# Layer 2's g product of a fused four-layer network: 128-column stationary tiles against pairs of 64-column tiles

## The chip, the cores and the metric

The kernel runs on one core of a Trainium2 chip. The metric is the device time of one execution in microseconds; the time before is the median of three runs. The engines are called PE (matrix products, with PEld for its weight loads), ACT, DVE, POOL and SP (whose queue issues most DMAs). A matrix product has a stationary operand (the "weight", loaded by LDWEIGHTS) and a moving operand that streams through the array; a shape such as 128\*64 after an instruction's name gives rows and columns of the part of the array that it uses, and 128x64 after that the moving operand. Each product of fp32 operands appears in the trace as two records (two passes), each with a weight load of its own.

## The reference

The input x is 4 samples of 256 channels of 48 x 48 pixels (N = 2304 pixels), fp32. Four layers follow one another, each adding its result for the group-normalised x to x: an attention with 8 heads of 64 (layer 0), a gate from max pooling and strip convolutions (layer 1), a non-local block (layer 2), and a channel gate with a 3 x 3 depthwise convolution (layer 3). The change lies in layer 2:

```python
xt = x.reshape(b, c, h * w)
theta_x = jnp.einsum('oc,bcn->bno', theta_w, xt) + theta_b
phi_x = jnp.einsum('oc,bcn->bon', phi_w, xt) + phi_b[:, None]
g_x = jnp.einsum('oc,bcn->bno', g_w, xt) + g_b
f = jnp.einsum('bnc,bcm->bnm', theta_x, phi_x) * c1 ** (-0.5)
attn = jax.nn.softmax(f, axis=-1)
y = jnp.einsum('bnm,bmc->bnc', attn, g_x)
```

theta, phi and g have 64 output channels each. g_x has the pixels in its rows, so its product takes the pixels of x as the stationary operand (transposed) and the weight g_w, 256 x 64, as the moving one.

## The kernel before, in words

Channels lie in 128 partitions and NK = 2 halves. Pixels are worked on in slices of SL = 384 (NSL = 6 to a sample). The order of the instructions on every engine is written out by hand: `attend` walks over groups of an attention unit (9 groups of two 128-pixel tiles each), and in each group records, in this order, the score products of the group (`scores`, L324, evicted by ACT with an exponential at L330 into `pt`), the jobs that fall due in it (`due`, `fills`, with ranks that order them), the "other" lanes of work (layer 1, norms), and the value products of the group before (`weigh`, L344). DVE and POOL add up the `pt` tiles (L370, L364; L355 on POOL). Layer 0 runs 16 phases of 6 units, layer 2 then 4 phases of 3 units.

`project2(b, norm, s2)` makes layer 2's operands of sample b. Per slice s it has two jobs:

- `both(s)`: theta and phi in one product of 128 output columns (L1199, two channel halves accumulated in one `pj` tile of PSUM), evicted by ACT in two halves (L1205, L1209), with a DMA copy of phi (L1213).
- `g(s)`: three tiles of 128 pixels, each the sum over two channel halves, into one `pj` tile (L1220); ACT copies the 128 x 192 result to `s2["v"]` (L1225). For sample 0 the next slice of x is fetched by a DMA afterwards (L1193).

`pj` tiles have two buffers, shared with every other small product: the output projection of layer 0 (`out_proj`, L723, two parts, read by DVE at L739), the sums of the softmax (`total`, L383, copied by ACT at L388; `total_here`, L429 in the last sample), the group means (L233, L247), and the per-channel statistics (L1255, read by DVE at L1263). A third tile of products can thus be begun only when the first has been read.

The jobs of the six slices are placed as follows. Sample 0: in the last phase of layer 0, one slice in each unit, in the order `both`, first part of the output projection, `g`, second part, `total`. Samples 1 and 2: in the layer-2 phase before, two slices at a time, in the order `both`, `both`, `g`, `g`. Sample 3: drained in one go at the end of sample 2's phase, slice by slice (`follow`), near 3190 to 3208 us in the trace. The start of `project2` computes biases, with two products into halves of the partitions (L1169, weights of 128 x 64, one moving column). Beside the layer-2 phases of samples 0 to 2, layer 1 of the last sample runs, on DVE (maxima, L890 to L922), PE (L1061), POOL and SP.

Of the kernel before, what the change touches and what calls it, by code (L numbers as in the profile page):

```python
# [14 lines left out]
P = 128  # L15
HW = 48
N = HW * HW
NK = 2
HEADS = 8
D = 64  # L20
# [58 lines left out]
def usual_path(  # L79
    tc, x, wqkv, wout, vecs, dww, thphi_w, thphi_b, g_w, g_b, W_w, attn_w1, attn_w2, refine_w, out  # L80
):
    nc = tc.nc
# [13 lines left out]
    def pj_tile():  # L96
        return ps_pj.tile([P, 512], F32, tag="pj", name="pj")
# [217 lines left out]
    HALVES = (slice(0, D), slice(D, P))  # L315
# [835 lines left out]
    def project2(b, norm, s2):  # L1151

        at = {}

        def start():
            kd = big.tile([P, N], F32, tag="k", name="kd")
            qv = big.tile([P, N], F32, tag="q", name="qv")
            s2["k"], s2["q"] = kd, qv[:, 0:HALF]
            s2["v"] = qv[:, HALF:N].rearrange("p (j d) -> p j d", d=D)
            ps = pj_tile()  # L1160

            for k in range(NK):
                nc.tensor.matmul(
                    ps[:, 0:1], lhsT=w2c[:, k, 0:2, :].rearrange("p t d -> p (t d)"),
                    rhs=norm["nb"][:, k : k + 1], start=k == 0, stop=k == NK - 1,
                )
            for c in HALVES:
                for k in range(NK):
                    nc.tensor.matmul(  # L1169
                        ps[c, 1:2], lhsT=w2c[:, k, 2, :],  # L1170
                        rhs=norm["nb"][:, k : k + 1], start=k == 0, stop=k == NK - 1,
                    )
            bias = small.tile([P, 2], F32, tag="bias2", name="bias2", bufs=3)
            nc.vector.tensor_add(bias, ps[:, 0:2], b2c)
            s2["shift"] = bias[:, 1:2]
            w = wqp.tile([P, NK, 3, P], F32, tag="w", name="w2")
            w = w.rearrange("p k t o -> p k (t o)")[:, :, : 3 * D]
            w = w.rearrange("p k (t d) -> p k t d", d=D)
            for k in range(NK):
                nc.scalar.activation(  # L1180
                    w[:, k], w2c[:, k], AF.Identity, scale=norm["rs"][:, k : k + 1]
                )
            if b:
                at["x"] = lambda s, k: X[b][:, k, s * SL : (s + 1) * SL]
            else:
                at["x"] = lambda s, k: at[s][:, k, :SL]
                fetch(0)
                fetch(1)
            at["w"], at["bias"] = w, bias

        def fetch(s):
            at[s] = xsp.tile([P, NK, SL + 1], F32, tag="xs", name="xs2")
            nc.sync.dma_start(at[s][:, :, :SL], x_out[:, :, s * SL : (s + 1) * SL])  # L1193

        def both(s):

            ps = pj_tile()[:, :SL]
            for k in range(NK):
                nc.tensor.matmul(  # L1199
                    ps, lhsT=at["w"][:, k, 0:2, :].rearrange("p t d -> p (t d)"),  # L1200
                    rhs=at["x"](s, k), start=k == 0, stop=k == NK - 1,
                )
            phi, theta = HALVES
            cols = slice(s * SL, (s + 1) * SL)
            nc.scalar.activation(  # L1205
                s2["k"][phi, cols], ps[phi], AF.Identity, bias=at["bias"][phi, 0:1]
            )
            c = s % L2C
            nc.scalar.activation(  # L1209
                s2["q"][HALVES[s // L2C], c * SL : (c + 1) * SL], ps[theta], AF.Identity,  # L1210
                bias=at["bias"][theta, 0:1],
            )
            nc.sync.dma_start(s2["k"][theta, cols], s2["k"][phi, cols])  # L1213

        def g(s):
            ps = pj_tile()
            nj = SL // P
            for i in range(nj):
                for k in range(NK):
                    nc.tensor.matmul(  # L1220
                        ps[:, i * D : (i + 1) * D],
                        lhsT=at["x"](s, k)[:, i * P : (i + 1) * P],
                        rhs=at["w"][:, k, 2, :], start=k == 0, stop=k == NK - 1,
                    )
            nc.scalar.copy(  # L1225
                s2["v"][:, s * nj : (s + 1) * nj, :].rearrange("p j d -> p (j d)"),
                ps[:, : nj * D],
            )
            if b == 0 and s + 2 < NSL:
                fetch(s + 2)  # L1230

        return start, [
            [(1, lambda s=s: both(s)), (2 if b else 2.7, lambda s=s: g(s))] for s in range(NSL)
        ]

# [225 lines left out]
    for i, (b, p) in enumerate(order):  # L1461
# [13 lines left out]
        else:  # L1475
            start, slices = project2(0, norms2[0], twos[0])
# [28 lines left out]
    for b in range(B):  # L1505
# [12 lines left out]
        if b + 1 < B:  # L1518
            spread(work, stats(b, 0), [22, 23])
            start, slices = project2(b + 1, norms2[b + 1], twos[b + 1])  # L1520
# [6 lines left out]
            at = [s for s in range(n) if s in work or s % NG == AT_TOTAL]  # L1527
# [147 lines left out]
    for k in range(NK):  # L1675
# [7 lines left out]
        of_groups, lhsT=gmat, rhs=means.rearrange("p b k -> p (b k)"), start=True, stop=True  # L1683
# [1350 lines left out]
```

## Time and profile before

| what | value |
|---|---|
| median of 3 runs | 3460.08 us (3459.35 to 3461.13) |
| profiled execution, own time | 3461.47 us |
| its span, first to last instruction | 3459.7 us |
| mean granted TensorE clock | 0.996 |
| PE busy | 3397.6 us (98%) |
| ACT, DVE, POOL busy | 66%, 73%, 24% |
| L1199 (`both`), PE busy | 35.7 us, 96 records |
| L1220 (`g`), PE busy | 35.3 us, 288 records |
| where L1220 runs | 2707 to 3208 us |

In the lines of the groups, the columns are the source line, the engine, the operation, the tiles written and read, the shape, the count, then busy time in us and the mean of one instruction in ns, then the idle time of the engine before them and what ended it. In the lines of a timeline, the first number is the start in us from the start of the span and the second the time that the merged instructions cover; the bracket gives idle time before and the releaser. A matrix product's recorded duration holds its latency, so the pace of a stream is read from the starts and not from the durations.

### The profile page before, as it was taken

Reading aid. Unit: us, or ns where it says so; the run is one execution under the profiler, and the core shown is the slowest. Engines: PE = TensorE matmul, PEld = TensorE weight load, DVE = VectorE, ACT = ScalarE, POOL = GpSimd, SP = SyncE. Lnnn points to the kernel's source line nnn. Section 1 sums busy time; section 2 is a strip of 40 time slices with the busy share of each in tenths; the row PEclk is TensorE's granted clock in tenths of the full one; section 3 lists DMA queues with packets and bytes.
Section 4 is the critical chain, followed back from the end, with each engine's and each line's share of the span. In section 5 each row is a group of like instructions: output and inputs, shape, how many; then the busy total and the mean of one; then the engine's idle time right before and its main releaser. Section 6 shows DMA issues by size and latency. Waiting matters only on the chain. (4 is left out here: it accounts for less than half of the span.)

```text
span 3459.7 us, 88715 instructions
## 1 busy us (share of the span) xinstructions
PE 3397.6 (98%) x37678; PEld 1711.7 (49%) x37678; DVE 2540.6 (73%) x3298; ACT 2297.1 (66%) x3690; POOL 824.9 (24%) x734
## 2 busy tenths in 40 slices
PE   8999999999999999999999999999999999899988
PEld 5555545555545444545454445554544444445533
DVE  3455545568788788687888787878887878857777
ACT  5565556565886687557866875568758855444577
POOL 2433333320011011101110010111011105776434
PEclk9999999999999999999999999999999999999999
DMA  2211111111111111121111110111111110221067
GB/s 91 49 23 27 22 27 22 27 22 27 21 32 22 27 22 27 27 72 22 27 22 27 15 31 15 31 18 31 18 28 17 30 21 9 59 62 11 8 152 230
DMA packets 111590, 127.20 MB, mean 37 GB/s; under 512 B 42912, under 2 KB 101648, under 8 KB 110416
## 3 DMA queue, kind: packets, MB, share of 16 engines
q1 hardware_dynamic: 109936, 119.53, 17.1%
q8 instruction: 297, 4.87, 0.6%
q10 hardware_dynamic: 1248, 1.91, 0.2%
q14 instruction: 109, 0.89, 0.1%
HBM read 56.99 MB, written 11.80 MB: 20 GB/s over the span
## 5 line engine op out<-in xcount | busy, mean ns | idle before, releaser
L330 ACT ACTIVATE pt<-sc 128x768 f32<-128x768 f32 x1944 | 1473.4, 810 | 759.8 <-PE sc L324 753.3
L370 DVE TENSOR_TENSOR acc<-acc,pt 128x768 f32<-128x768 f32 x1368 | 1367.1, 999 | 145.5 <-ACT pt L330 51.8
L344 PE MATMUL av<-pt,v 64*64 64x384 f32 x13824 | 1274.9, 484 | 0.0
L324 PE MATMUL sc<-q,k 64*64 64x384 f32 x13824 | 1270.1, 482 | 0.5 <-ACT pt L330 0.5
L324 PEld LDWEIGHTS sc<-q,k 64*64 64x64 f32 x13824 | 525.4, 133 | 589.6 <-issue 556.5
L344 PEld LDWEIGHTS av<-pt,v 64*64 64x64 f32 x13824 | 518.2, 133 | 568.4 <-issue 521.5
L421 POOL TENSOR_TENSOR o<-o,rinv 128x384 f32<-128x384 f32 x95 | 120.3, 1267 | 1712.4 <-DMA rinv<-rinv 1702.4
L355 POOL TENSOR_TENSOR half<-pt 128x768 f32<-128x768 f32 x189 | 369.0, 1957 | 495.2 <-ACT pt L330 417.0
L739 DVE SCALAR_TENSOR_TENSOR x<-pj,bo,x 128x384 f32<-128x384 f32 x192 | 118.5, 617 | 346.3 <-ACT row L388 188.0
L951 ACT ACTIVATE prod<-pd,wt 128x256 f32<-128x256 f32 x486 | 340.7, 761 | 0.2
L370 DVE TENSOR_TENSOR acc<-acc,half 128x768 f32<-128x768 f32 x171 | 187.6, 1097 | 169.4 <-POOL half L355 168.2
L625 PE MATMUL pj<-xs,w 128*128 128x384 f32 (+1 forms) x720 | 275.4, 505 | 0.0
L625 PEld LDWEIGHTS pj<-xs,w 128*128 128x128 f32 x720 | 124.1, 189 | 127.9 <-ACT v L664 34.3
L974 DVE TENSOR_REDUCE prod<-prod 128x256 f32<-128x1280 f32 x114 | 168.7, 1480 | 0.9 <-ACT prod L951 0.9
L344 PE MATMUL av<-pt,qv 64*64 64x384 f32 x1728 | 169.0, 495 | 0.0
L324 PE MATMUL sc<-qv,kd 64*64 64x384 f32 x1728 | 165.3, 487 | 2.3 <-ACT pt L330 2.2
L723 PE MATMUL pj<-o,wo 128*128 128x384 f32 (+1 forms) x384 | 161.3, 502 | 1.1 <-DVE x L739 0.8
L364 DVE TENSOR_TENSOR acc<-pt 128x768 f32<-128x768 f32 x99 | 119.7, 1209 | 39.3 <-ACT pt L330 39.1
L659 PEld LDWEIGHTS pj<-w,xs 128*128 128x128 f32 x1080 | 134.4, 191 | 24.2 <-issue 1.2
L659 PE MATMUL pj<-w,xs 128*128 128x128 f32 x1080 | 134.9, 275 | 0.0
L417 POOL TENSOR_TENSOR o<-raw 128x384 f32<-128x384 f32 x95 | 120.8, 1271 | 45.9 <-ACT raw L413 44.7
L413 ACT COPY raw<-av 128x768 f32<-128x768 f32 x108 | 86.4, 800 | 48.3 <-PE av L344 47.8
(304 smaller groups left out, 2256.4 us busy)
## 6 DMA issues: line engine op xcount, KB each, us to landing
xs<-in_x_dram SPq DMA_DIRECT2D x90, 384.0 KB
sh<-pad SPq DMA_DIRECT2D x126, 162.2 KB
rinv<-rinv SPq DMA_DIRECT2D x208, 94.5 KB
out_dram<-x SPq DMA_DIRECT2D x23, 384.0 KB
w<-in_wqkv_dram SPq DMA_DIRECT2D x32, 192.0 KB
x<-in_x_dram SPq DMA_DIRECT2D x4, 1152.0 KB
x<-in_x_dram SPq DMA_DIRECT2D x9, 384.0 KB
rinv<-ls SPq DMA_DIRECT2D x208, 1.5 KB
```

The lines of the kernel that those rows point to most:

```text
L324: nc.tensor.matmul(ps[c * D : (c + 1) * D, h, :SL], lhsT=u["of"]["k"][r, j0 : j0 + D], rhs=u["of"]["q"][r, u["qc"]], start=True, stop=True,)
L330: nc.scalar.activation(pt, ps[:, :, :SL], AF.Exp, scale=u["scale"])
L344: nc.tensor.matmul(u["av"][h * D : (h + 1) * D, half, :SL], lhsT=value(u, j, h)[r], rhs=pt[r, h, :], start=j == 0, stop=j == JB - 1,)
L355: nc.gpsimd.tensor_add(half, pts[0], pts[1])
L370: nc.vector.tensor_add(u["acc"], u["acc"], term)
L417: eng.tensor_add(u["sum"], u["raw"][:, 0, :], u["raw"][:, 1, :])
L421: eng.tensor_mul(o, o, u["rinv"])
L625: nc.tensor.matmul(ps[:, :n], lhsT=at["w"][:, k, t, :], rhs=xs[s][:, k, :n], start=k == 0, stop=k == NK - 1,)
L659: nc.tensor.matmul(ps[:, i * P : (i + 1) * P], lhsT=xs[s][:, k, i * P : (i + 1) * P], rhs=at["w"][:, k, 2, :], start=k == 0, stop=k == NK - 1,
L723: nc.tensor.matmul(ps[:, :n], lhsT=wo[:, p, k * P : (k + 1) * P], rhs=o["o"][:, :n], start=True, stop=True,)
L951: nc.scalar.activation(bufs[n % 3][:, :, min(n, 1) + i].rearrange("p (r c) -> p r c", c=AS), pd[:, PAD + dr : PAD + dr + AS, PAD + dc : PA ...
L974: nc.vector.tensor_reduce(to, bufs[n % 3][:, :, : min(n, 1) + len(taps)], AX.X, ALU.add)
```

## The change

In `g`, each stationary operand of 128 pixels is given as two stationary operands of 64 pixels, one after the other, with the same moving operand; the second writes PSUM partitions 64 to 127. `HALVES` is `(slice(0, 64), slice(64, 128))`. The sums, the `pj` tile and the copy that follows are as they were.

```diff
             for i in range(nj):
                 for k in range(NK):
-                    nc.tensor.matmul(
-                        ps[:, i * D : (i + 1) * D],
-                        lhsT=at["x"](s, k)[:, i * P : (i + 1) * P],
-                        rhs=at["w"][:, k, 2, :], start=k == 0, stop=k == NK - 1,
-                    )
+                    for c in HALVES:
+                        nc.tensor.matmul(
+                            ps[c, i * D : (i + 1) * D],
+                            lhsT=at["x"](s, k)[:, i * P + c.start : i * P + c.stop],
+                            rhs=at["w"][:, k, 2, :], start=k == 0, stop=k == NK - 1,
+                        )
```

## The prediction

> **What bounds the kernel now.** I read the page's engine table first, then the groups by shape for the edited line, then the timeline at each place where that line runs, and the waits of PE between those places.
>
> ```profile
> PE 3397.6 (98%) x37678; PEld 1711.7 (49%) x37678; DVE 2540.6 (73%) x3298; ACT 2297.1 (66%) x3690; POOL 824.9 (24%) x734
> L1220 PE MATMUL pj<-w,x 128*128 128x64 f32 x216 | 26.0, 275 | 0.0
> L1220 PE MATMUL pj<-w,xs 128*128 128x64 f32 x72 | 9.3, 279 | 3.7 <-ACT qv L1209 3.7
> ```
>
> PE sets the time. The edited line has 288 records: 24 calls of g with 12 each (three 128-pixel tiles, two channel halves, and two passes per fp32 product). They hold 35.3 us, so no more can be at stake. The trace starts one of them every 112 ns: in the next timeline 12 weight loads fill 1.42 us, and (1420 - 192) / 11 = 112. The moving part is only 64 columns, and 112 ns is also the pace of L659, which moves 128. So the load of a 128-column weight sets this pace. The 24 calls stand in three surroundings. The first, six times in the last phase of layer 0:
>
> ```profile
> 2707.03 0.58 ACT L1209 ACTIVATE qv<-pj,bias 64x384 f32<-64x384 f32 x1
> ...
> 2707.65 1.42 PEld L1220 LDWEIGHTS pj<-w,xs 128*128 128x128 f32 x12 [1.24 <-ACT qv L1209]
> 2707.66 1.55 PE L1220 MATMUL pj<-w,xs 128*128 128x64 f32 x12 [0.62 <-ACT qv L1209]
> 2708.99 0.30 PEld L723 LDWEIGHTS pj<-o,wo 128*128 128x128 f32 x2
> ```
>
> PE stands 0.62 us until ACT has evicted `both`, does g, and goes straight on to L723. The second, six pairs of calls in layer 2 (the first of two timeline fences), and the third, six calls drained one after another near 3200 us (the second):
>
> ```profile
> 2903.74 2.89 PE L1220 MATMUL pj<-w,x 128*128 128x64 f32 x24
> ...
> 2904.40 0.58 ACT L1209 ACTIVATE qv<-pj,bias 64x384 f32<-64x384 f32 x1
> ...
> 2906.56 0.21 PEld L344 LDWEIGHTS av<-pt,qv 64*64 64x64 f32 x8
> ```
>
> ```profile
> 3192.34 1.45 PE L1220 MATMUL pj<-w,x 128*128 128x64 f32 x12
> ...
> 3193.14 0.58 ACT L1209 ACTIVATE qv<-pj,bias 64x384 f32<-64x384 f32 x1
> ...
> 3193.77 1.56 PE L1199 MATMUL pj<-x,w 128*128 128x384 f32 x4
> ```
>
> In the pair, the second call may start when the second eviction ends, 2904.40 + 0.58 + 0.05 = 5.03 (counting from 2900); before, PE arrived at 5.13. In the third surrounding the next `both` starts 50 ns after ACT's L1209 ends: PE already waits for ACT there, whatever g takes.
>
> **What the Trainium skill says.** "TensorE: Matmul & The Clock Gate", section "LDWEIGHTS (loading the stationary operand)", prices a load by its columns over 1.2 GHz: 107 ns for 128 and 53 for 64. The trace's 112 agrees for 128, with some 5 ns of handover. "TensorEngine Tiling (Array Packing)", section "Key Properties", says that tiles load and multiply independently, and that a change of tiling drains the engine. Both show in the trace:
>
> ```profile
> 2701.75 0.32 PEld L1169 LDWEIGHTS pj<-gn_nb,w2c 128*64 128x64 f32 x8
> 2701.75 0.41 PE L1169 MATMUL pj<-gn_nb,w2c 128*64 128x1 f32 x8
> ...
> 3238.30 0.20 PEld L429 LDWEIGHTS pj<-acc,ones 128*64 128x64 f32 x4 [0.60 <-issue]
> 3238.31 0.87 PE L429 MATMUL pj<-acc,ones 128*64 128x384 f32 x4
> ```
>
> L1169 loads 128x64 weights into two column tiles: 8 loads of 138 ns in 0.32 us, in pairs 13 ns apart, one pair each (320 - 138 - 13) / 3 = 56 ns (58 between its products). In L429 the two halves stream 384 columns together (starts 7 ns apart, then 373 ns on). The drain: L383 of 128x32 tiles starts its last product at 2710.130, streams 96 columns for 80 ns, and the 64x64 tiles of L344 start loading at 2710.304, 94 ns later; L429 gives 94 as well. "TensorE: Matmul & The Clock Gate", section "The mechanism" under Part 3, says that a load overlaps running products only for another row group; L1169 and L659 (load and product of 107 ns each at a pace of 112) use the same rows and do overlap, so the measurement decides for me.
>
> **The change part by part.** Each call's 12 loads and products of 128*128 become 24 of 128*64, two column tiles side by side. PSUM contents, the copy L1225, ACT, DVE, POOL and the DMAs keep their number and order; only lines of PE grow (288 loads and 288 products more).
> - Inside a call, before: from first to last product 1277 ns (160 for the first, exposed load, then 10 x 111.7). After: 109 ns for the first interval (53 of exposed load and 56 of products), then 10 x 58, and 7 for the second half: 696. Saved: 581 ns. A 64-column pace between 56 (products) and 62 (some handover more) moves this by -20 to +40 ns.
> - Change of tiling on the way in: the drain of 94 ns ends before the eviction that g waits for (0.62 us of idle; in the pairs the load starts 465 ns after L1199's last product, the drain would allow it at 320 + 94 = 414). Cost nothing while that wait is there. Only the third surrounding has no such wait: 94 + 53 of exposed load.
> - On the way out: to L723 the next load may start 53 + 94 = 147 ns after the last product instead of 56: 91 lost, or 87 with rounding of the starts. To L344 (64x64) the drain is paid already: nothing.
>
> First surrounding: 581 - 87 = 494 ns a call. The fourth call is followed by L723 waiting for DVE's L739 until 2796.02, 0.24 us of idle, so its gain is lost: 5 x 0.494 = 2.47 us. PE's own later waits here (DVE L443 near 2882) hang on PE's L429 and move along.
>
> Pairs: before, from the first product to the last 1277 + 111 + 1229 = 2617 ns. After, the first call ends early but the second waits for the eviction, 5.03 - 3.74 = 1.29 us, and then takes 0.70: 1.99. Gain 0.63 us a pair, half of what the pair saves on PE. The pairs at 2903 and 2935 lie in a stretch where DVE has no gap from 2890.6 to 2984, but for some 0.1 us thrice, and PE waits for it after each:
>
> ```profile
> 2919.89 1.73 DVE L243 TENSOR_TENSOR gn_sq<-gn_sq,gn_mv 128x2 f32<-128x2 f32 x1
> ...
> 2921.68 0.38 PE L247 MATMUL pj<-gn_sq,gmat 128*128 128x2 f32 x2 [1.05 <-DVE gn_sq L243]
> ```
>
> ```profile
> 2952.16 1.25 PE L324 MATMUL sc<-qv,kd 64*64 64x384 f32 x12 [2.20 <-ACT pt L330]
> ```
>
> I take both gains as lost to these waits, which grow by 0.63 us. From 2984 on DVE itself waits for POOL's L355, which waits for ACT and so for PE, 15 times at L370 alone up to 3192: there a gain stays. Four pairs: 2.50 us.
>
> Third surrounding: five calls gain nothing (ACT's two evictions, 0.58 each, set the cycle of 2.83 us). The last is followed by L344: before, its last product starts 322 + 1173 = 1495 ns after L1199's last; after, 414 + 2 + 696 = 1112. Gain 0.38 us.
>
> Sum: 2.47 + 2.50 + 0.38 = 5.35 us. The profiled execution took 3461.47 us (span 3459.7, 1.8 around it), 1.4 above the median 3460.08 of the runs. It should become 3456.1; taken from the median, 3454.7. What the sum leaves out is the granted clock: after 2880 us the trace has six stretches at half clock (the shortest 3.41 us, the window that "TensorE: Matmul & The Clock Gate" gives in "What's actually happening"), a window each worth up to 1.7 us of PE, and a shift of PE can move one in or out. So 1.7 either way.
>
> **The rivals.**
> A, more arrives. DVE's L243 took 1.73 us for 128x2 while POOL ran L355 beside it (other DVE lines of that shape take 0.16). If such stretches end with POOL, whose start follows PE, the waits at 2921 and 2952 move along, and the two lost pairs come back; the fourth call of the first surrounding does too if DVE reaches L739 sooner: 5.35 + 1.25 + 0.49 = 7.1 us, 3453.0. For it: the length of L243. Against: DVE's row has no gap, so its backlog stays.
>
> B, less arrives. DVE's stretches beside POOL fall otherwise in the later pairs too and eat their 2.50: 2.85 us, 3457.2. Against it: 4 to 7 us gaps in DVE's row after 2984.
>
> C, slower. The halves don't overlap, since nothing in this trace alternates 64-column loads with products as short as 64 columns in column tiles. With load and product of both halves in a row, a pair costs 4 x 53 + 10 = 222 ns: a call takes 2.44 us. First surrounding 5 x 1.25 + 0.8; pairs 4 x 2.6, and 2.0 for the two whose waits take the rest; third 5 x 1.3 + 1.4: 27 us, 3487. It decides from about 108 ns a pair, where nothing is gained, and passes 0.2% at about 137. Loads alone in a row (117) would give about no change. Against it: L1169 and L429.
>
> **How the numbers follow.** 0.2% of the time, 6.9 us, is about what a measurement of this kernel can tell from no change. Forecast 0.46, A 0.33, B 0.13, C 0.08. With 1.7 us of clock either way, A passes 6.9 us in somewhat over half of its cases and the forecast in some 0.17 of its own: 0.22 + 0.08 = 0.30 faster. C gives slower nearly always, 0.08; the rest, 0.62, is within 0.2%. The range runs from A with the clock's gain and a little more of the saved 581 ns (9 us, 3451.0) to B with the clock's loss (3459.0); C and some ends of A lie outside.
>
> **What would show it.** L1220 as 128*64, 576 records, 24 of them in about 0.97 us with the last one's tail, pairs 58 ns apart; L723 loading 147 ns after the last product; PE waiting about 0.5 us for L1209 between the two calls of a pair; a cycle of 2.83 us unchanged near 3200; and waits at 2921 and 2952 longer by 0.6 (shorter ones speak for A). A pair interval over 100 ns makes the forecast wrong, and so does a wait of PE for DVE after 2984 that grows by a call's gain.

## The result, and the profile after

The changed kernel takes 3453.76 us in the median, the kernel before 3461.89 in the same comparison; the medians lie 8.1 us apart. The ratio, for which an interval is given, is 0.9979 (95%: 0.9973 to 0.9984), so 7.3 us faster (5.5 to 9.3). The forecast was 5.35. The profiled execution took 3453.34 us with a span of 3451.5, 8.2 shorter than the profiled span before.

From the page's engine table and the groups by shape (samples 1 to 3 of the edited line, now L1221):

```profile
PE 3384.6 (98%) x37966; PEld 1698.6 (49%) x37966; DVE 2539.3 (74%) x3298; ACT 2297.4 (67%) x3690; POOL 828.0 (24%) x734
L1221 PE MATMUL pj<-w,x 128*64 128x64 f32 x432 | 16.5, 226 | 2.2 <-ACT qv L1209 2.2
```

PE has 288 products more and is busy for 13.0 us less. Before, half as many records of these samples filled 26.0 us. The last entry is new: PE now waits for ACT's L1209 inside the pairs. The timelines of the three surroundings, first the first call in layer 0's last phase:

```profile
2708.17 0.78 PEld L1221 LDWEIGHTS pj<-w,xs 128*64 128x64 f32 x24 [1.24 <-ACT qv L1209]
2708.18 0.92 PE L1221 MATMUL pj<-w,xs 128*64 128x64 f32 x24 [0.62 <-ACT qv L1209]
2709.02 0.30 PEld L723 LDWEIGHTS pj<-o,wo 128*128 128x128 f32 x2
```

24 loads in 0.78 us where 12 took 1.42; the idle of 0.62 ahead is as before, and L723 loads 0.85 us after the first load, not 1.34. Then a pair in layer 2, and the drained calls:

```profile
2900.83 0.58 ACT L1209 ACTIVATE qv<-pj,bias 64x384 f32<-64x384 f32 x1
...
2901.46 0.92 PE L1221 MATMUL pj<-w,x 128*64 128x64 f32 x24 [0.37 <-ACT qv L1209]
2902.30 0.21 PEld L344 LDWEIGHTS av<-pt,qv 64*64 64x64 f32 x8
```

```profile
3186.40 0.58 ACT L1209 ACTIVATE qv<-pj,bias 64x384 f32<-64x384 f32 x1
...
3187.03 1.56 PE L1199 MATMUL pj<-x,w 128*128 128x384 f32 x4 [0.42 <-ACT qv L1209]
```

The second call of the pair stands until 50 ns after the eviction ends. In the drained calls the next `both` does the same as before; its idle, too short to be shown before, is now 0.42 us: what g saves there goes into this wait.

**Where it came from.** ACT's L330 (one instruction for each tile of scores) is the same in every kernel here, so the difference of its starts between two traces is the shift of the whole schedule. Minus is earlier than the kernel before; the columns are places in that kernel's time.

```text
near (us)        2700   2862   2892   2912   2925   2984   3025   3058   3098   3188   3212   3295   end
changed         +0.52  -1.93  -3.57  -4.25  -3.65  -4.47  -5.14  -5.81  -6.50  -6.74  -7.18  -7.18  -8.13
first six       +0.13  -2.33  -3.96  -3.96  -4.06  -4.06  -2.71  -2.65  -2.64  -4.21  -4.05  -4.06  -5.75
pairs           +0.16  +0.16  +0.23  -0.46  +0.18  -0.48  -1.19  -1.84  -2.55  -2.99  -3.00  -3.01  -3.49
drained         +0.21  +0.22  +0.22  +0.22  +0.13  +0.10  +1.71  +1.71  +1.72  +0.35  +0.01   0.00  +0.01
again           +0.29  -2.16  -3.79  -4.48  -3.87  -4.57  -5.25  -5.92  -6.58  -6.97  -7.42  -7.42  -8.27
```

In the changed kernel: 2.45 us by the sixth call (2700 to 2862); 0.68 at each pair, the first given back by 2925 and the second before 2984; 0.44 at the last drained call (3188 to 3212). With four pairs that is 5.6 us. The other steps (1.64 us gained between 2862 and 2892, 0.24 between 3098 and 3188, 0.95 after 3295) belong to no call. The first of them is a stretch in which the granted clock was half; here the same 14 us in the kernel before, then in the changed one (columns: span, busy time and count of PE, PEld, DVE, ACT, POOL, granted clock, DMA share, GB/s):

```profile
2878.00:2892.00 14.00, 12.50 (x102) 5.57 (x98) 9.77 (x16) 3.82 (x6) 7.26 (x6) 0.88 0.00 1
```

```profile
2878.00:2892.00 14.00, 12.50 (x122) 6.04 (x122) 11.45 (x20) 5.18 (x9) 9.04 (x6) 1.00 0.01 2
```

A clock of 0.88 over 14 us is one stretch of 3.41 us at half clock. The clock theory of the expectations below is about it.

### The profile page after: what moved, and what is told of

Same layout as the page of the kernel before. It is cut to its first block, busy times and chain, and to the rows that moved or that the text cites. A ratio compares the mean times of both kernels' runs of the same rounds, so it can differ in the third digit from the quotient of the medians.

```text
span 3451.5 us, 89291 instructions
## 1 busy us (share of the span) xinstructions
PE 3384.6 (98%) x37966; PEld 1698.6 (49%) x37966; DVE 2539.3 (74%) x3298; ACT 2297.4 (67%) x3690; POOL 828.0 (24%) x734
## 5 line engine op out<-in xcount | busy, mean ns | idle before, releaser
L330 ACT ACTIVATE pt<-sc 128x768 f32<-128x768 f32 x1944 | 1473.6, 810 | 757.9 <-PE sc L324 751.4
L344 PE MATMUL av<-pt,v 64*64 64x384 f32 x13824 | 1274.8, 484 | 0.0
L344 PEld LDWEIGHTS av<-pt,v 64*64 64x64 f32 x13824 | 518.2, 133 | 568.4 <-issue 521.5
L739 DVE SCALAR_TENSOR_TENSOR x<-pj,bo,x 128x384 f32<-128x384 f32 x192 | 118.5, 617 | 344.2 <-ACT row L388 186.9
L344 PE MATMUL av<-pt,qv 64*64 64x384 f32 x1728 | 167.1, 490 | 0.0
L723 PE MATMUL pj<-o,wo 128*128 128x384 f32 (+1 forms) x384 | 161.4, 502 | 2.3 <-DVE x L739 2.0
```

Of the source, the lines that this page charges most:

```text
L330: nc.scalar.activation(pt, ps[:, :, :SL], AF.Exp, scale=u["scale"])
L344: nc.tensor.matmul(u["av"][h * D : (h + 1) * D, half, :SL], lhsT=value(u, j, h)[r], rhs=pt[r, h, :], start=j == 0, stop=j == JB - 1,)
L723: nc.tensor.matmul(ps[:, :n], lhsT=wo[:, p, k * P : (k + 1) * P], rhs=o["o"][:, :n], start=True, stop=True,)
```

## Experiments

**Parts of the change.** Each of three kernels makes the halves for some samples alone:

```diff
-                    for c in HALVES:
+                    for c in HALVES if b == 0 else (slice(0, P),):      # first six
+                    for c in HALVES if b in (1, 2) else (slice(0, P),): # pairs
+                    for c in HALVES if b == 3 else (slice(0, P),):      # drained
```

First six calls:

> Two column tiles for sample 0's six calls alone (in layer 0's last phase); the other 18 calls as before. Waits theory (a call gains 0.494 us where nothing else holds PE, the fourth gains nothing): 2.47 us off by the end of the sixth call, near 2855. Clock theory (half-clock stretches lie on a fixed grid of 3.41 us and follow a window in which PE did little; a shift of 2 us moves PE's poor stretch at 2880 across a boundary of it): no half-clock stretch at 2883, so 1.6 us more, 4.1 in all near 2890 and about that at the end. If the missing stretch of the changed kernel was chance, it stands at 2883 again and the total is 2.5.

Pairs:

> Two column tiles for samples 1 and 2 alone (the six pairs of calls). Waits theory: each pair gains 0.63 us, those near 2904 and 2936 give it back at PE's next wait for DVE, so 2.5 us in all. Rival A (DVE's stretched instructions follow PE through POOL): all six stay, 3.75 us. Clock theory adds: PE comes to 2880 as before, so a half-clock stretch stands at 2883, and the gain carries no clock bonus there.

Drained calls:

> Two column tiles for sample 3 alone (six calls drained in a row near 3192 to 3208). Waits theory: the cycle of 2.83 us stays, since ACT's two evictions set it, and the last call alone gains 0.38 us: no change that can be measured. If g's length counted in that cycle, 6 x 0.38 = 2.3 us.

Measured ratios to the kernel before: 0.9994 (0.9986 to 1.0002), 0.9991 (0.9985 to 0.9998) and 0.9998 (0.9989 to 1.0006); the three sum to 5.9 us. The intervals are too wide to tell one small part; the shifts are not. The first six give 2.46 us by 2862, the pairs 0.68 or 0.69 each (the one at 2904 returned by 2925, the one at 2936 before 2984), the drained calls 0.34. So the waits theory holds for each part, and rival A's 3.75 us for the pairs does not. The waits of PE that absorb the first two pairs grew by 0.60 and 0.57 us in the changed kernel (its timeline; the second reaches PE through ACT, whose L330 stands behind an L934 that waits for DVE's L933):

```profile
2918.03 0.38 PE L247 MATMUL pj<-gn_sq,gmat 128*128 128x2 f32 x2 [1.65 <-DVE gn_sq L243]
...
2948.39 0.92 PE L324 MATMUL sc<-qv,kd 64*64 64x384 f32 x4 [2.77 <-ACT pt L330]
```

**Halves one after the other.** The loop over `HALVES` is moved outside those over `i` and `k`.

```diff
-            for i in range(nj):
-                for k in range(NK):
-                    for c in HALVES:
+            for c in HALVES:
+                for i in range(nj):
+                    for k in range(NK):
```

> All calls in 128 x 64 parts, but all twelve passes of the first half of the columns before those of the second, so that neighbours in program order use the same column tile. If products start in program order, the halves do not overlap: 24 x 58 = 1.39 us a call, 0.1 more than before, and with the change of tiling 0.2 us lost in the first surrounding and nothing gained elsewhere: 1 to 2 us slower than before. If PE takes later products for a free tile first, it runs as the changed kernel, 0.70 us a call.

Measured 0.9995 (0.9986 to 1.0003), so not the 1 to 2 us slower that I expected. The timeline shows both calls of a pair as one run of records:

```profile
2902.54 2.59 PEld L1221 LDWEIGHTS pj<-w,x 128*64 128x64 f32 x48 [0.59 <-ACT qv L1209]
2902.54 2.72 PE L1221 MATMUL pj<-w,x 128*64 128x64 f32 x48
```

From first to last product a call takes 1211 ns, against 696 in the changed kernel and 1277 before: passes of one half follow each other 58 ns apart, and only where the second half begins do records lie beside the end of the first. The records do not name their half; read by their pace, the second half's first three start 169, 63 and 4 ns before the first half's last. By 2862 the six calls have cost 0.12 us together (+0.32 to +0.44); the pairs gain 0.17 each. So products of the two tiles start in program order but for a look ahead of about three, and the halves run side by side through a whole call only where neighbours in that order alternate. I had the call at 1.39 us: the overlap at the seam was not in the sum. The shift of -1.02 at 3295 holds the 1.64 us of clock, which this profile has too.

**The granted clock.** The question is whether the half-clock stretch near 2883 hangs on when PE gets there. The kernel before, and the changed one, with 2.0 us of idle products (`hum`, whose result is not read) at 2701:

```diff
             ps = pj_tile()
+            if b == 0:
+                hum(ps[:, P : 2 * P], 9)
```

On the kernel before:

> The kernel before with nine idle products of 128 columns (18 passes of 112 ns, 2.0 us) on PE just before layer 2's bias products at 2701, whose result is not read. PE is the bound there, so without the clock the time grows by 2.0 us. Clock theory: everything near 2880 comes 2.0 us later, its poor stretch is split by the grid, and the half-clock stretch at 2883 is gone: 2.0 - 1.6 = 0.4 us slower near 2890. At the end other stretches may have moved as well.

On the changed kernel:

> The changed kernel with the same 2.0 us of idle products at 2701. It comes to 2880 about when the kernel before does. Clock theory: the half-clock stretch at 2883 comes back, so near 2890 it is 2.0 + 1.6 = 3.6 us behind the changed kernel. Without a fixed grid: 2.0 behind, with or without the stretch.

Measured 1.0007 (0.9999 to 1.0016) and 0.9993 (0.9985 to 1.0001). The same view of 14 us for the kernel before with idle products, and for the changed one:

```profile
2878.00:2892.00 14.00, 12.57 (x94) 4.63 (x86) 7.71 (x12) 5.64 (x9) 6.53 (x5) 0.88 0.00 1
```

```profile
2878.00:2892.00 14.00, 12.50 (x102) 5.56 (x98) 9.80 (x16) 3.83 (x6) 6.95 (x5) 0.88 0.01 2
```

Both have a half-clock stretch. A grid that is fixed to the start of the program falls. In the kernel before the stretch did not go: it came 2 us later (2885.43 instead of 2883.47), and the schedule was exactly 2.0 us late at 2892. In the changed kernel it came back, as the theory had said, but the grid itself had moved: the starts of the stretches, modulo 3.413 us (the phase of the grid), are at 2.61 in the kernel before, 1.16 and 2.80 in these two. They agree within a profile to 2 ns and differ between profiles, in the kernels of this study from 0.36 to 3.33. By the medians the change is worth 5.1 us with idle products in both kernels (3462.86 and 3457.80).

**The changed kernel again.**

> The changed kernel once more, for the granted clock. Free grid: its half-clock stretches lie at another phase than in the first profile, the steps of the calls are the same (0.49 a call, 0.68 a pair, 0.4 at the end: 5.6 us), and the ends of the two profiles differ by the stretches alone. Fixed grid: the phase is 2.60 us again and the stretches are where they were.

Ratio 0.9980 (0.9971 to 0.9989), median 3453.72. The phase is 2.21 us (2.60 in the first profile), the calls' steps are the same to 0.05 us (the row "again" above), and the stretches happen to lie in the same places as in the first profile (none near 2883), so the ends agree as well.

**Without the wait for the eviction.** `both` writes into scores tiles, which leaves both `pj` tiles to g. First with one tile for the two slices of a pair, g in the old and in the new form:

```diff
-            ps = pj_tile()[:, :SL]
+            if not b or s < L2C:
+                at["sc"] = sc_tile()
+            ps = at["sc"][:, s // L2C if b else 0, :SL]
```

Old form:

> The kernel before, with the products of both written into a scores tile of PSUM (for samples 1 to 3 the two slices of a pair in the two banks of one tile) instead of a pj tile, so that g no longer waits for ACT's eviction; g in 128-column tiles. Expected against before: the 0.62 us of idle ahead of each of the first six calls goes (5 x 0.7), the pairs gain 0.1 each, the last surrounding's cycle falls from 2.83 to about 2.62 us: 5 us faster. If the scores of the next group then wait for that tile, it is no faster.

New form:

> The same with g in pairs of 64-column tiles. If the eviction is what took half of the pairs' gain and all of the drained calls', the change is now worth 0.3 us in each of the first six calls, 1.1 in a pair (four of them), 0.3 in each drained call: 8 us against the same kernel with 128-column tiles, so 13 us faster than before. If something else took it (DVE, issue), 5 us against it as in the changed kernel.

Measured 1.0010 (1.0003 to 1.0016) and 0.9989 (0.9981 to 0.9997): a miss. The timeline of the old form, second `both` of a pair:

```profile
3016.48 1.56 PE L1201 MATMUL sc<-x,w 128*128 128x384 f32 x4 [1.27 <-ACT qv L1211]
```

It waits 1.27 us for the eviction of the first, although that lies in another bank: it seems that the order which the program keeps goes by tile. So the wait was only moved. Each `both` with a tile of its own takes it away:

```diff
-            ps = pj_tile()[:, :SL]
+            ps = sc_tile()[:, 0, :SL]
```

Old form:

> The kernel before, with each product of both in a scores tile of its own (two of them in turn), g in 128-column tiles. If the second product of a pair waited only because it shared a tile with the first, that wait is gone: the first six calls gain 2.6 us as in the kernel with the shared tile, the pairs 0.1 each, the drained calls' cycle falls from 2.83 to 2.62 us: 3.5 to 4 us faster than before. If scores tiles are what is short, PE waits at the scores after a pair, and it is no faster.

New form:

> The same with g in pairs of 64-column tiles. Eviction theory: without the wait for L1209 a pair gains 1.3 us (four of the six stay), the first six calls 0.8 each but for the fourth, a drained call 0.5: 12 us faster than before, so 8 us against the same kernel with 128-column tiles. If DVE or the issue of instructions had taken the gain instead, the pairs stay at 0.7 and the sum at 8 to 9.

Measured 0.9992 (0.9986 to 0.9999), 2.8 us faster than before, and 0.9968 (0.9956 to 0.9980), 11 us faster. The pair of the new form:

```profile
2900.70 1.62 PE L1221 MATMUL pj<-w,x 128*64 128x64 f32 x48
2902.24 0.21 PEld L344 LDWEIGHTS av<-pt,qv 64*64 64x64 f32 x8
```

Two calls follow each other without a gap, and L344 comes 1.54 us after their first product, where it came 2.82 before and 2.13 in the changed kernel. The steps are 3.85 us in the first six calls, 0.91 in a pair, 2.88 in the drained calls, whose cycle is now 2.34 us. The first and third are as expected; the pair was expected to give 1.3, and most of the rest is a new wait of 0.34 us ahead of its first `both`, for ACT to read the scores out of that tile:

```profile
2897.92 2.85 PE L1199 MATMUL sc<-x,w 128*128 128x384 f32 x8 [0.34 <-ACT pt L330]
```

The old form has this wait too, and its steps are 2.57 us in the first six calls, a loss of 0.17 in a pair and 0.82 in the drained calls. So the eviction did hold back the change: by the steps of one profile each, with four pairs, the halves are now worth 7.7 us (10.4 less 2.7), where they were worth 5.6 and 8 were expected. The whole times can't show this. The medians of the last two kernels (3458.47 and 3451.64, the second from six times) lie 6.8 us apart, those of the changed kernel and the kernel before 8.1.

Last, with g ahead of the sums in the first six calls:

```diff
-            [(1, lambda s=s: both(s)), (2 if b else 2.7, lambda s=s: g(s))] for s in range(NSL)
+            [(1, lambda s=s: both(s)), (2 if b else 4.05, lambda s=s: g(s))] for s in range(NSL)
```

> As the kernel with scores tiles and 64-column parts, and in the first surrounding g stands after the second part of the output projection, directly ahead of the 128x32 tiles of the sums: one change of tiling less a call. Expected: the drain and the exposed load on the way out, 0.15 us or a little more in each of six calls, 0.9 us: 13 us faster than before. If the second part of the output projection then waits (its pj tile), nothing.

Measured 0.9964 (0.9951 to 0.9978), median 3448.61. The steps of the first six calls are 3.83 us, no more than without it. The timeline shows what took the place of the change of tiling:

```profile
2736.54 0.78 PEld L1221 LDWEIGHTS pj<-w,xs 128*64 128x64 f32 x24 [0.68 <-DVE x L739]
```

g now needs the `pj` tile that L739 reads last. Both new forms with a scores tile for each `both` lie below the changed kernel in the median; a gain of the second over the first is not shown, since their intervals against the kernel before overlap.

## Why the prediction was right, and where it was off

- **Inside a call.** 696 ns from first to last product were forecast; 696 or 697 are in the trace in all 24 calls. The page "TensorE: Matmul & The Clock Gate" prices a 64-column load at 53 ns ("LDWEIGHTS (loading the stationary operand)"), the L1169 row gave 58 with the handover, and 58 it is, now with 64 moving columns. Rival C is out, but the experiment with the halves one after the other shows on what it hung: their order in the program.
- **Changes of tiling.** 147 ns from the last product to the next load were forecast on the way out, 150 measured (to L723 and L344 alike). On the way in, 416 ns after L1199's last product in the drained calls, as worked out.
- **First surrounding.** 0.494 us a call forecast, 0.49 measured; the fourth call's gain went into the wait for L739, whose idle rose from 0.24 to 0.88 us.
- **Pairs.** 0.63 forecast, 0.68 measured. The term that was mis-sized is the way out to L344, which I took as unchanged: it fell from 203 to 150 ns. I read that from the records so: before, the last product's record starts 56 ns after that of its load, and loads follow each other every 112 ns, so that about half of the load still lay ahead of the product; a load of 64 columns is over by then. The same 53 ns make the last drained call 0.44 instead of 0.38 (0.34 where the drained calls alone were changed).
- **What swallows.** The two pairs near 2904 and 2936 were lost to DVE, as forecast; DVE's stretched L243 (1.73 us in both kernels) did not carry the gain on. Rival B is out too: all four later pairs kept theirs.
- **The rest.** The steps make 5.6 us and the interval of the ratio begins at 5.5. Its middle, 7.3, is 1.7 us more. In the two profiled executions the rest is mostly granted clock: the half-clock stretch at 2883 (1.64 us) is in the profile before and not in the two of the changed kernel. It is missing too with the first six calls alone, with the halves one after the other and with the shared scores tile in the new form, and present in the other kernels, three of which have halves in the first six calls. What orders these fourteen profiles is where the grid lies under the work. In the time of the kernel before (grid less the shift at 2862), a stretch of the grid that begins between 2882.9 and 2884.2 is at half clock in nine profiles of ten, the exception being the first six calls alone; in the other four profiles the grid has no beginning there (they lie at 2881.5 to 2882.0 and 3.41 us later), and none of them shows the stretch. Between the two profiles compared here the phase is the same to 12 ns, so there the shift decided. From execution to execution the phase moves (the window is free-running in the words of "TensorE: Matmul & The Clock Gate", "What's actually happening", and the phases agree), so the 1.64 us of these profiles are most likely luck of the phase and no lasting part of the gain. The other executions point the same way: the mean granted clock is 0.9962 over 130 of the kernel before and 0.9961 over 31 of the changed one (standard errors 0.0001 and 0.0002), where one stretch fewer would add 0.0005. What, if anything, makes the whole gain larger than the steps stays open. The last 160 us add a scatter of their own: with the same instructions they were from 1.7 us shorter to 2.8 longer than in the profile before.
- **The number.** That 3453.76 lies only 0.9 us from the forecast 3454.7 is in part luck: the median of three from which it was taken, 3460.08, is 1.8 below the 3461.89 of the comparison, and the gain was 1.9 us (by the ratio) or 2.8 (by the medians) larger than forecast. Taken alone, the number would speak for rival A (3453.0, 7.1 us), whose two lost pairs did not come back; the parts tell the two apart, the sum does not. A gain above 6.9 us had a chance of 0.30 and one below it 0.62. The 0.22 in that sum is two thirds of A's 0.33; "somewhat over half" would be about 0.18.

## What to carry to other kernels

Where the moving operand is short, the load of the stationary one sets the pace, and halving it into two column tiles that alternate in program order nearly halves the time (1277 to 696 ns here); count one drain and one exposed load at each border to another tiling that no wait covers. What it is worth is decided outside: list, at each place, the wait that comes next on PE, and ask whether its releaser follows PE or its own backlog. Here evicting from another pool's tiles took the steps from 5.6 us to 10.4; 2.7 of them come with the old form of g as well.

## What the runs showed of the hardware

A weight load overlaps running products of the same rows in another column tile (in L429 two loads of 136 ns, 7 ns apart, while products of both tiles stream). Products of two column tiles start nearly in program order: twelve passes of one tile ahead of twelve of the other took 1211 ns, with three records of the second tile ahead of the first's last, and alternating passes took 696. From the start of the last 64-column product to the first load of another tiling there are 150 ns. The half-clock stretches lie on a grid of 3.413 us that is fixed to 2 ns within an execution and differs between executions (2.60 and 2.21 us in two of the same kernel).
